# The second node stage of a two-layer graph network on Trainium2: its order of work written out step by step, with rows fetched into six buffers

## The chip, the cores and the metric

The kernel runs on one core of one Trainium2 chip. The metric is device time in microseconds (us). Before the change it is 3491.12 us, the median of three runs from 3474.59 to 3492.3. All times of parts come from one profiled execution of the kernel, whose own time is 3487.8 us and whose span is 3486.0 us.

A core has five engines with a queue of instructions each: PE (matrix multiply, with its weight loads shown as PEld), DVE (vector), ACT (scalar functions), POOL (general purpose, issues the indirect transfers here) and SP (issues transfers).[...]

## The reference, cut to what matters

Two layers of a graph network act on 6250 nodes with 256 features and 100000 edges. The first, `_L0_gnn_ref`, ends with a stage per node, and the second, `_L1_gnn_ref`, begins with one. In the reference, with `t` the mean of the messages at a node and `x` the normalised input:

```python
trans = typed_linear(t, Wa, ba)              # one of 3 matrices, by the node's type
alpha = sigmoid(skip)[node_type][:, None]
out = trans * alpha + x * (1.0 - alpha)
normed = (out - mu) * rsqrt(var + LN_EPS) * ln_g[node_type] + ln_b[node_type]
L0 = where(has_msg, normed, x)
x = x0 + L0                                  # x0: the kernel's input
h = maximum(_layernorm(x), 0.0)              # second layer's input
xw = h @ W                                   # and its two attention sums per head
```

The kernel computes exactly these lines, per block of nodes, in the stage that is changed. After it, the second layer gathers rows of `xw` for every edge.

## The kernel before, in words

**Stages.** A first node stage makes keys, values and queries and writes the table `hq_d`. A first edge stage gathers 832 groups of key and value rows and sums messages into `QA`, an array in SBUF (its first 256 columns are `acc0`). The second node stage, L1342 to L1442, is the one in question. A second edge stage (from L1451) gathers 832 groups of rows of `xw_d`, sums them into `acc1`, and a last stage normalises over all nodes. Each edge stage ends with a part under a run-time condition; at such a condition all engines meet. So the second node stage starts with all engines free, and from there to the end of the second edge stage's fixed part the instructions are one pool that the planner may order.

**The second node stage.** The 6250 nodes are cut into 50 blocks of 127 (`NB`, `BN`). For each block, `block(b)` (L1372) does, in four pieces separated by `yield`:

1. loads rows of `x` into `xbuf` and of `hq_d` into `hbuf` (`load_rows`, L170, two transfers each because 127 rows are cut into 112 and 15); clears and loads a tile with the types of the nodes (`load_types`, L183; POOL memset L187, transfer L188); gathers the three per-type rows (scale, offset, skip) into `norm` (an indirect transfer on POOL, L971, with three buffers); turns the block's message sums with PE (L197) and multiplies them by the mask of each of the three types (`by_type`, L193; DVE, L200, three instructions called `tm`); makes `xh` on ACT (L1384) and adds `x` to it on POOL (L1385).
2. twelve matmul instructions on PE for the six products with `wa_s` (L1390); on DVE the skip term `o` (L1395), `o` plus product (L1396), mean and variance (`norm_stats`, L151: statistics L154 and L156, the square root on ACT L158, the reciprocal on DVE L159), and the two instructions of the normalisation (L1398, L1399).
3. `xn` on DVE (L1402), its statistics, `shift` (L1405), the relu `h2` on ACT (L1407), the sum `r` on POOL (L1409) and its store to `r_d` (SP, L177).
4. two transposes of `h2` (PE, L1414), a copy to SBUF (ACT, L1416), the next layer's rows (PE, four instructions, L1419), three copies (ACT, L1421 to L1424) and the store to `xw_d` (SP).

**What sets the order.** A loop starts one block per round and advances up to three blocks by one piece each, oldest last. This is only the order in which the instructions are handed over. The stage is not under a fixed order: the planner that builds the program orders each engine's instructions by what its own estimate says is ready, and lets later code of the same region move ahead. `xbuf` and `hbuf` have four slots, everything else three (`wk`), and one PSUM pool of eight banks serves all PSUM tiles.

After the loop, DVE turns the attention sums into `es` and `adst` (L1434 to L1442), and the second edge stage begins: `acc1` is cleared on DVE (L1453), and its first gathers (POOL, L971, `rows<-xw_d`) follow.

Of the kernel before, what the change touches and what calls it, by code (L numbers as in the profile page):

```python
# [24 lines left out]
def kernel(  # L25
# [122 lines left out]
    kind_at = pers.tile([P, NB], I32, name="kind_at")  # L148


    def norm_stats(pool, a, tag):  # L151

        st = pool.tile([P, nc.vector.BN_STATS_DIM], F32, name="st_" + tag)
        nc.vector.bn_stats(out=st, in_=a)  # L154
        mv = pool.tile([P, nc.vector.BN_AGGR_DIM], F32, name="mv_" + tag)
        nc.vector.bn_aggr(out=mv, in_=st)  # L156
        rs = pool.tile([P, 1], F32, name="rs_" + tag)
        nc.scalar.activation(rs, mv[:, 1:2], AF.Sqrt, bias=eps_t)  # L158
        nc.vector.reciprocal(rs, rs)  # L159
        return mv[:, 0:1], rs  # L160

    def rows_of(b):
        return LAST if b == NB - 1 else BN

# [5 lines left out]
    def load_rows(t, a, b):  # L170

        for o, e in pieces(rows_of(b)):
            nc.sync.dma_start(t[o + 1 : e + 1], a[b * BN + o : b * BN + e, :])

    def store_rows(a, b, t, eng=None):
        for o, e in pieces(rows_of(b)):
            (eng or nc.sync).dma_start(a[b * BN + o : b * BN + e, :], t[o + 1 : e + 1])  # L177

    def by_block(a, some):

        return a[some, :].rearrange("(b p) d -> p b d", p=BN)

    def load_types(pool, b):  # L183

        t = pool.tile([P, P], I32, name="ntype")
        n = rows_of(b)
        nc.gpsimd.memset(t, -1)  # L187
        nc.sync.dma_start(  # L188
            t[:, 1 : n + 1], bass.AP(tensor=node_type.tensor, offset=node_type.offset + b * BN, ap=[[0, P], [1, n]])
        )  # L190
        return t

    def by_type(pool, psum, a, nt, tag):  # L193

        ps = psum.tile([P, FC, P], F32, name="nps")
        for c in range(FC):
            nc.tensor.transpose(ps[:, c, :], a[:, c * P : (c + 1) * P], ident)  # L197
        m = pool.tile([P, T, FC, P], F32, name=tag)
        for t in range(T):
            nc.vector.scalar_tensor_tensor(  # L200
                m[:, t], nt[:, None, :].to_broadcast([P, FC, P]), float(t), ps, op0=OP.is_equal, op1=OP.mult
            )
        return m

# [765 lines left out]
    def gather(to, table, index):  # L970
        nc.gpsimd.indirect_dma_start(  # L971
            out=to, out_offset=None, in_=table[:, :], in_offset=bass.IndirectOffsetOnAxis(ap=index, axis=0)
        )
# [368 lines left out]
    with ExitStack() as st:  # L1342
        cst = st.enter_context(tc.tile_pool(name="e0c", bufs=1))
        wk = st.enter_context(tc.tile_pool(name="e0w", bufs=3))
        pp = st.enter_context(tc.tile_pool(name="e0p", bufs=8, space=PSUM))
        wa_s = load_w(cst, Wa, "wa_s")


        gw_s = cst.tile([P, FC, D], F32, name="gw_s")
        nc.scalar.dma_start(gw_s, gW.rearrange("(c p) o -> p c o", p=P))  # L1350
        asd = cst.tile([P, 2, D], F32, name="asd")
        nc.scalar.dma_start(asd[:, 0, :], bcast(att_src, D))
        nc.scalar.dma_start(asd[:, 1, :], bcast(att_dst, D))
        gwx = cst.tile([P, FC, H * XW + H], F32, name="gwx")
        by_head = gwx[:, :, : H * XW].rearrange("p c (h e) -> p c h e", h=H)
        for c in range(FC):
            nc.scalar.copy(by_head[:, c, :, :DK], gw_s[:, c, :].rearrange("p (h e) -> p h e", h=H))
            pr = wk.tile([P, 2, H, DK], F32, name="pr")
            nc.vector.tensor_tensor(
                pr.rearrange("p i h e -> p i (h e)"), gw_s[:, c, None, :].to_broadcast([P, 2, D]), asd, op=OP.mult  # L1360
            )
            nc.vector.tensor_reduce(by_head[:, c, :, DK], pr[:, 0], AX.X, OP.add)
            nc.vector.tensor_reduce(gwx[:, c, H * XW :], pr[:, 1], AX.X, OP.add)
        a_sd = cst.tile([P, NB, 2, H], F32, name="a_sd")

        XB = 4
        xbuf = cst.tile([P, XB, D], F32, name="xbuf")
        hbuf = cst.tile([P, XB, D], F32, name="hbuf")
        nc.gpsimd.memset(xbuf, 0.0)
        nc.gpsimd.memset(hbuf, 0.0)  # L1370

        def block(b):  # L1372

            xb = xbuf[:, b % XB, :]
            load_rows(xb, x, b)
            nt = load_types(wk, b)
            hb = hbuf[:, b % XB, :]
            load_rows(hb, hq_d[:, :D], b)
            norm = wk.tile([P, 3, D], F32, name="norm")
            gather(norm.rearrange("p i d -> p (i d)"), norm_d, kind_at[:, b : b + 1])  # L1380
            m = by_type(wk, pp, acc0[:, b, :D], nt, "tm")

            xh = wk.tile([P, D], F32, name="xh")
            nc.scalar.activation(xh, hb, AF.Copy, scale=nhas[:, b : b + 1])  # L1384
            nc.gpsimd.tensor_tensor(xh, xh, xb, op=OP.add)  # L1385
            yield
            tr = pp.tile([P, D], F32, name="nps")
            for t in range(T):
                for c in range(FC):
                    nc.tensor.matmul(  # L1390
                        tr, m[:, t, c, :], wa_s[:, t, c, :],
                        start=(t == 0 and c == 0), stop=(t == T - 1 and c == FC - 1),
                    )
            o = wk.tile([P, D], F32, name="o")
            nc.vector.scalar_tensor_tensor(o, hb, nalpha[:, b : b + 1], norm[:, 2, :], op0=OP.mult, op1=OP.add)  # L1395
            nc.vector.scalar_tensor_tensor(o, tr, share[:, b : b + 1], o, op0=OP.mult, op1=OP.add)  # L1396
            mean, rs = norm_stats(wk, o, "o")
            nc.vector.scalar_tensor_tensor(o, o, mean, norm[:, 0, :], op0=OP.subtract, op1=OP.mult)  # L1398
            nc.vector.scalar_tensor_tensor(o, o, rs, norm[:, 1, :], op0=OP.mult, op1=OP.add)  # L1399
            yield  # L1400
            xn = wk.tile([P, D], F32, name="xn")
            nc.vector.scalar_tensor_tensor(xn, o, has[:, b : b + 1], xh, op0=OP.mult, op1=OP.add)  # L1402
            mean, rs = norm_stats(wk, xn, "x")
            shift = wk.tile([P, 1], F32, name="shift")
            nc.vector.tensor_scalar(shift, mean, rs, -1.0, op0=OP.mult, op1=OP.mult)  # L1405
            h2 = wk.tile([P, D], F32, name="h2")
            nc.scalar.activation(h2, xn, AF.Relu, bias=shift, scale=rs)  # L1407
            r = wk.tile([P, D], F32, name="r")
            nc.gpsimd.tensor_tensor(r, xn, h2, op=OP.add)  # L1409
            store_rows(r_d, b, r)  # L1410
            yield
            hp = pp.tile([P, FC, P], F32, name="nps")
            for c in range(FC):
                nc.tensor.transpose(hp[:, c, :], h2[:, c * P : (c + 1) * P], ident)  # L1414
            hT = wk.tile([P, FC, P], F32, name="hT")
            nc.scalar.copy(hT, hp)  # L1416
            wp = pp.tile([P, H * XW + H], F32, name="nps")
            for c in range(FC):
                nc.tensor.matmul(wp, hT[:, c, :], gwx[:, c, :], start=(c == 0), stop=(c == FC - 1))  # L1419
            xw = wk.tile([P, H, XW], F32, name="xw")  # L1420
            nc.scalar.copy(xw.rearrange("p h e -> p (h e)"), wp[:, : H * XW])  # L1421
            store_rows(xw_d, b, xw.rearrange("p h e -> p (h e)"))
            nc.scalar.copy(a_sd[:, b, 0, :], xw[:, :, DK])
            nc.scalar.copy(a_sd[:, b, 1, :], wp[:, H * XW :])  # L1424

        parts = []
        for b in range(NB + 3):
            if b < NB:
                parts.append(block(b))
            for p in parts[::-1]:  # L1430
                next(p, None)
            parts = parts[-3:]

        es = cst.tile([P, NB, 2 * H], F32, name="es")  # L1434
        nc.vector.tensor_copy(es[:, :, :H], a_sd[:, :, 1, :])
        nc.vector.tensor_add(es[:, :, H:], a_sd[:, :, 0, :], a_sd[:, :, 1, :])
        nc.vector.scalar_tensor_tensor(es[:, :, H:], es[:, :, H:], 0.2, es[:, :, H:], op0=OP.mult, op1=OP.max)
        for i in range(3):
            nc.vector.tensor_copy(adst[:, :, i, :], es)
            if i < 2:  # L1440
                nc.vector.tensor_tensor(es, es, adst[:, :, i, :], op=OP.subtract)
# [463 lines left out]
```

## Time and profile before

The stage lies between 1818 and about 2128 us of the span. For three parts of it (us):

| from : to | PE busy | DVE busy | ACT busy | POOL busy | granted PE clock | DMA share |
|---|---|---|---|---|---|---|
| 1818.0 : 1845.0 | 14.06 | 15.38 | 4.80 | 10.29 | 0.66 | 0.65 |
| 1845.0 : 2100.0 | 201.29 | 209.77 | 111.78 | 121.48 | 0.97 | 0.64 |
| 2100.0 : 2128.7 | 10.03 | 20.83 | 5.61 | 2.27 | 0.60 | 0.08 |

| whole execution | |
|---|---|
| its own time | 3487.8 us |
| span | 3486.0 us |
| median of the runs | 3491.12 us |
| busy in the span | PE 67%, DVE 72%, ACT 54%, POOL 60% |

How to read the lines that follow. A row in order of time gives start, duration, engine, line, operation, `output<-inputs`, shapes, a count, and in brackets how long the engine had been idle and what ended that wait. An engine name with a `q` (SPq, ACTq) is the issuing of a transfer by that engine's queue. Matmuls overlap each other, so a busy PE is not a PE at its peak. Two DVE rows may overlap by about 0.1 us[...].

### The profile page before, as it was taken

The numbers are of one execution on the slowest core, as the hardware profiler recorded it, in microseconds if no ns is written. First come the engines' busy times: TensorE is split into PE (matmuls) and PEld (weight loads), VectorE is DVE, ScalarE is ACT, GpSimd is POOL, SyncE is SP. The second block draws the span as 40 slices with busy tenths as digits, with TensorE's granted clock in tenths as the row PEclk, the third lists the DMA queues.
The fourth block names the chain that finished last, engine by engine and source line by source line (L and its number), as shares of the span: only waits on it lengthen the run. The fifth ranks groups of instructions, "written<-read, shape, count | busy, mean of one in ns | idle before, by whom it ended". The sixth has DMA issues, their size and how long they took to land. (4 is left out here: it accounts for less than half of the span.)

```text
span 3486.0 us, 45931 instructions
## 1 busy us (share of the span) xinstructions
PE 2321.6 (67%) x9879; PEld 1626.8 (47%) x9879; DVE 2501.3 (72%) x5600; ACT 1884.6 (54%) x7331; POOL 2105.7 (60%) x2144
## 2 busy tenths in 40 slices
PE   3888765787777777777767772465555556556680
PEld 2555543555555555555536662344344334434440
DVE  8998705898898988889858884455555555555688
ACT  5665561776677777677764441444444444444511
POOL 4665555676666666666614444777777777777300
PEclk9899887998899999999989995677877877777855
DMA  3555687676666767666626663444444444444224
GB/s 99 232 210 219 205 273 222 202 215 198 196 193 199 210 204 206 193 199 207 197 76 171 178 177 103 127 126 129 126 123 127 125 123 128 125 125 127 56 77 132
DMA packets 263729, 571.80 MB, mean 164 GB/s; under 512 B 66395, under 2 KB 162193, under 8 KB 257194
## 3 DMA queue, kind: packets, MB, share of 16 engines
q0 software_dynamic: 124368, 444.93, 41.9%
q1 hardware_dynamic: 131838, 116.55, 12.3%
q10 hardware_dynamic: 7238, 7.22, 0.8%
q8 instruction: 94, 1.54, 0.2%
q14 instruction: 191, 1.56, 0.1%
HBM read 458.42 MB, written 114.06 MB: 164 GB/s over the span
## 5 line engine op out<-in xcount | busy, mean ns | idle before, releaser
L971 POOL DMA_INDIRECT ring<-kv_d,idx x832 | 820.3, 986 | 438.4 <-ACT wrows L1230 184.7
L971 POOL DMA_INDIRECT rows<-xw_d,idx x832 | 873.2, 1049 | 260.8 <-issue 203.8
L1230 ACT ACTIVATE wrows<-ring,wt 128x64 f32<-128x64 f32 x3328 | 834.2, 335 | 0.1
L1713 PE MATMUL aps<-wrows,ebn 128*128 128x264 f32 x1664 | 605.1, 505 | 301.9 <-DVE ebn L1689 151.4
L1074 PE MATMUL qe<-QA,nbe 128*128 x1664 | 467.6, 415 | 170.7 <-DVE nbe L1059 102.5
L1295 PE MATMUL aps<-wrows,ebn 128*128 128x258 f32 x1664 | 520.4, 422 | 38.9 <-ACT wrows L1230 31.7
L1713 PEld LDWEIGHTS aps<-wrows,ebn 128*128 128x128 f32 x1664 | 350.3, 237 | 383.5 <-ACT wrows L1675 332.9
L1074 PEld LDWEIGHTS qe<-QA,nbe 128*128 128x128 f32 x1664 | 330.5, 207 | 265.4 <-issue 165.6
L1675 ACT ACTIVATE wrows<-rows,ex 128x64 f32<-128x64 f32 x1664 | 434.2, 336 | 0.0
L1295 PEld LDWEIGHTS aps<-wrows,ebn 128*128 128x128 f32 x1664 | 318.2, 206 | 131.3 <-ACT wrows L1230 80.7
L1086 DVE TENSOR_TENSOR pr<-ring,qe 128x512 f32<-128x512 f32 x416 | 277.3, 679 | 133.1 <-PE qe L1074 65.8
L1532 ACT COPY asr<-rows 128x16 f32<-128x16 f32 x208 | 44.8, 216 | 575.1 <-DMA rows<-xw_d,idx 575.1
L1729 DVE TENSOR_TENSOR acc<-acc,aps 128x264 f32 x416 | 176.8, 425 | 192.2 <-PE aps L1713 178.0
L1089 DVE TENSOR_REDUCE att<-pr 128x8 f32<-128x512 f32 x416 | 268.7, 677 | 0.1
L1239 DVE SCALAR_TENSOR_TENSOR QA<-QA,same,aps 128x258 f32 x416 | 194.1, 467 | 43.3 <-PE aps L1295 39.4
L578 ACT COPY QA<-rps 128x768 f32<-128x768 f32 x204 | 163.8, 803 | 88.2 <-PE rps L577 85.2
L1577 DVE TENSOR_TENSOR e<-asr,ad 128x128 f32<-128x128 f32 x26 | 10.1, 388 | 215.1 <-ACT asr L1532 215.1
L1390 PE MATMUL nps<-wa_s,tm 128*128 128x256 f32 x600 | 146.6, 397 | 9.2 <-DMA norm<-norm_d,kind_at 6.4
L447 POOL DMA_INDIRECT kv_d<-QA,to_row x51 | 56.7, 1112 | 148.1 <-ACT QA L578 141.5
L1553 PEld LDWEIGHTS <-near 128*128 128x128 bf16 x832 | 96.8, 118 | 102.1 <-issue 41.9
L1689 DVE TENSOR_TENSOR ebn<-ifree,dl 128x512 f32<-128x512 f32 x208 | 142.7, 686 | 0.0
L1208 DVE TENSOR_TENSOR ebn<-ifree,dl 128x512 f32<-128x512 f32 x208 | 140.7, 676 | 2.8 <-PE aps L1295 2.8
(438 smaller groups left out, 3947.3 us busy)
## 6 DMA issues: line engine op xcount, KB each, us to landing
near<-row_d SPq DMA_DIRECT2D x208, 128.0 KB
near<-row_d SPq DMA_DIRECT2D x52, 512.0 KB
ring<-kv_d,idx POOLq DMA_INDIRECT x832
rows<-xw_d,idx POOLq DMA_INDIRECT x832
keeps<-prev_d SPq DMA_DIRECT2D x416, 16.0 KB
xw_d<-xw SPq DMA_DIRECT2D x49, 113.8 KB
xbuf<-xw_d SPq DMA_DIRECT2D x49, 113.8 KB
xbuf<-in_x_dram SPq DMA_DIRECT2D x49, 112.0 KB
```

The costliest lines, as they stand in the source:

```text
L578: nc.scalar.copy(rel[:, :, i, 2 * c : 2 * c + 2, :].rearrange("p r h e -> p h r e"), ps)
L971: nc.gpsimd.indirect_dma_start(out=to, out_offset=None, in_=table[:, :], in_offset=bass.IndirectOffsetOnAxis(ap=index, axis=0))
L1074: nc.tensor.matmul(qe[:, i, :], oh[j // GT][:, j % GT + i, :], QA[:, 1:, :D][:, bass.ds(bs[j // 2], 1), :].rearrange("p a d -> p (a d)"), ...
L1086: nc.vector.tensor_tensor(pr.rearrange("p t h e -> p t (h e)"), ring[:, lane : lane + 2, slot(t), :], qe, op=OP.mult)
L1089: nc.vector.tensor_reduce(att[:, :, k + j : k + j + 2].rearrange("p h t -> p t h"), pr, AX.X, OP.add)
L1230: nc.scalar.activation(wv[:, j % GT, cols], v[:, cols], AF.Copy, scale=w[:, h, j : j + 1])
L1239: nc.vector.scalar_tensor_tensor(a, a, same[:, t : t + 1], sums.pop(j), op0=OP.mult, op1=OP.add),
L1295: nc.tensor.matmul(sums[j - j % 2], hot[j // GT][:, j % GT, :], wvs[j // GT][:, j % GT, :], start=(j % 2 == 0), stop=(j % 2 == 1),)
L1390: nc.tensor.matmul(tr, m[:, t, c, :], wa_s[:, t, c, :], start=(t == 0 and c == 0), stop=(t == T - 1 and c == FC - 1),)
L1675: nc.scalar.activation(wv[:, part, h, :DK], rows[:, part, h, :DK], AF.Copy, scale=ex[:, 0, h, g * GT + part : g * GT + part + 1],)
L1713: nc.tensor.matmul(sums[t - t % 2], oh[:, t % GT, :], wv[:, t % GT].rearrange("p h e -> p (h e)"), start=(t % 2 == 0), stop=(t % 2 == 1),)
L1729: nc.vector.tensor_tensor(a, a, sums.pop(t).rearrange("p (h e) -> p h e", h=H), op=OP.add)
```

## The change

The stage is put under a fixed order: inside it each engine issues its instructions in the order in which they are written. Where the stage's instructions fall among others of the same engine that are written outside it stays with the planner. The pieces of a block become twelve functions, and a step calls each for another block. Rows, types and per-type rows are fetched three steps ahead into six slots (`tbuf`, `nbuf`, `xbuf`, `hbuf`); the types' slots are cleared once instead of once per block. The PSUM pool has two buffers for each of four tiles instead of eight for all. The reciprocal of each standard deviation moves behind the next DVE instruction(s). The two stores to `xw_d` are issued by ACT instead of SP. The computations themselves, and their shapes, stay.

```diff
-        pp = st.enter_context(tc.tile_pool(name="e0p", bufs=8, space=PSUM))
+        pp = st.enter_context(tc.tile_pool(name="e0p", bufs=2, space=PSUM))
...
-        XB = 4
+        AHEAD = 3
+        XB = AHEAD + 3
...
+        tbuf = cst.tile([P, XB, P], I32, name="tbuf")
+        nbuf = cst.tile([P, XB, 3, D], F32, name="nbuf")
...
+        def fetch_rows(b):
+            i = b % XB
+            n = rows_of(b)
+            nc.sync.dma_start(
+                tbuf[:, i, 1 : n + 1],
+                bass.AP(tensor=node_type.tensor, offset=node_type.offset + b * BN, ap=[[0, P], [1, n]]),
+            )
+            load_rows(hbuf[:, i, :], hq_d[:, :D], b)
+            load_rows(xbuf[:, i, :], x, b)
+            gather(nbuf[:, i].rearrange("p i d -> p (i d)"), norm_d, kind_at[:, b : b + 1])
...
+        def added(b):
+            i = b % XB
+            xh = live["xh", b] = wk.tile([P, D], F32, name="xh")
+            nc.scalar.activation(xh, hbuf[:, i, :], AF.Copy, scale=nhas[:, b : b + 1])
+            nc.gpsimd.tensor_tensor(xh, xh, xbuf[:, i, :], op=OP.add)
...
+        def norm_of(b):
+            i = b % XB
+            o = live["o", b]
+            mean, rs = live.pop(("so", b))
+            nc.vector.scalar_tensor_tensor(o, o, mean, nbuf[:, i, 0, :], op0=OP.subtract, op1=OP.mult)
+            nc.vector.reciprocal(rs, rs)
+            nc.vector.scalar_tensor_tensor(o, o, rs, nbuf[:, i, 1, :], op0=OP.mult, op1=OP.add)
...
+            store_rows(xw_d, b, xw.rearrange("p h e -> p (h e)"), nc.scalar)
...
-        parts = []
-        for b in range(NB + 3):
-            if b < NB:
-                parts.append(block(b))
-            for p in parts[::-1]:
-                next(p, None)
-            parts = parts[-3:]
+        with tc.manual_schedule():
+            for step in range(-AHEAD, NB + 4):
+                for back, part in (
+                    (AHEAD, fetch_rows),
+                    (1, added),
+                    (2, turn_sums),
+                    (1, masks),
+                    (-3, rows_of_next),
+                    (-2, turn_rows),
+                    (1, products),
+                    (1, skips),
+                    (0, sums_in),
+                    (-1, joined),
+                    (0, norm_of),
+                    (-1, rows_out),
+                ):
+                    if 0 <= step + back < NB:
+                        part(step + back)
```

By engine, a step is then: DVE `masks` (three `tm`), `skips`, `sums_in` (the product added to `o`, and its statistics), `joined` (`xn` and its statistics), `norm_of` (two instructions with the reciprocal between), `rows_out` (reciprocal and `shift`). POOL: the gather, the addition of `xh`, the addition of `r`. ACT: `xh`, the copy `xw` with its two stores, two small copies, the copy `hT`, two square roots, the relu. PE: `turn_sums`, `rows_of_next`, `turn_rows`, `products`. SP: five loads and the two stores to `r_d`.

More of the change, by code (lines that the diff above doesn't have):

```diff
@@ L148 @@
     kind_at = pers.tile([P, NB], I32, name="kind_at")
[L151 to L160, printed above, removed]
     def rows_of(b):
@@ L181, in by_block @@
         return a[some, :].rearrange("(b p) d -> p b d", p=BN)
[L183 to L203, printed above, removed]
     qapool = tc.tile_pool(name="qapool", bufs=1)
@@ L1364, with turn_sums, masks, products @@
         a_sd = cst.tile([P, NB, 2, H], F32, name="a_sd")
-        XB = 4
+        AHEAD = 3
+        XB = AHEAD + 3
         xbuf = cst.tile([P, XB, D], F32, name="xbuf")
         hbuf = cst.tile([P, XB, D], F32, name="hbuf")
+        tbuf = cst.tile([P, XB, P], I32, name="tbuf")
+        nbuf = cst.tile([P, XB, 3, D], F32, name="nbuf")
         nc.gpsimd.memset(xbuf, 0.0)
         nc.gpsimd.memset(hbuf, 0.0)
[L1372 to L1387, printed above, removed]
+        nc.gpsimd.memset(tbuf, -1)
+        live = {}
+        def fetch_rows(b):
[8 more added lines that the diff above has]
+            gather(nbuf[:, i].rearrange("p i d -> p (i d)"), norm_d, kind_at[:, b : b + 1])
+        def turn_sums(b):
+            ps = live["sums", b] = pp.tile([P, FC, P], F32, name="sums_ps")
+            for c in range(FC):
+                nc.tensor.transpose(ps[:, c, :], acc0[:, b, c * P : (c + 1) * P], ident)
+        def masks(b):
+            ps = live.pop(("sums", b))
+            m = live["tm", b] = wk.tile([P, T, FC, P], F32, name="tm")
+            nt = tbuf[:, b % XB, :]
+            for t in range(T):
+                nc.vector.scalar_tensor_tensor(
+                    m[:, t], nt[:, None, :].to_broadcast([P, FC, P]), float(t), ps, op0=OP.is_equal, op1=OP.mult
+                )
+        def products(b):
+            m = live.pop(("tm", b))
+            tr = live["tr", b] = pp.tile([P, D], F32, name="tr_ps")
             for t in range(T):
@@ L1393, in block @@
                     )
[L1394 to L1403, printed above, removed]
+        def skips(b):
+            i = b % XB
+            o = live["o", b] = wk.tile([P, D], F32, name="o")
+            nc.vector.scalar_tensor_tensor(
+                o, hbuf[:, i, :], nalpha[:, b : b + 1], nbuf[:, i, 2, :], op0=OP.mult, op1=OP.add
+            )
+        def added(b):
[3 more added lines that the diff above has]
+            nc.gpsimd.tensor_tensor(xh, xh, xbuf[:, i, :], op=OP.add)
@@ new lines, in spread, with sums_in @@
+        def spread(a, tag):
+            st_ = wk.tile([P, nc.vector.BN_STATS_DIM], F32, name="st_" + tag)
+            nc.vector.bn_stats(out=st_, in_=a)
+            mv = wk.tile([P, nc.vector.BN_AGGR_DIM], F32, name="mv_" + tag)
+            nc.vector.bn_aggr(out=mv, in_=st_)
+            rs = wk.tile([P, 1], F32, name="rs_" + tag)
+            nc.scalar.activation(rs, mv[:, 1:2], AF.Sqrt, bias=eps_t)
+            return mv[:, 0:1], rs
+        def sums_in(b):
+            o = live["o", b]
+            nc.vector.scalar_tensor_tensor(
+                o, live.pop(("tr", b)), share[:, b : b + 1], o, op0=OP.mult, op1=OP.add
+            )
+            live["so", b] = spread(o, "o")
@@ new lines, in norm_of, with joined @@
+        def norm_of(b):
+            i = b % XB
+            o = live["o", b]
+            mean, rs = live.pop(("so", b))
+            nc.vector.scalar_tensor_tensor(o, o, mean, nbuf[:, i, 0, :], op0=OP.subtract, op1=OP.mult)
+            nc.vector.reciprocal(rs, rs)
+            nc.vector.scalar_tensor_tensor(o, o, rs, nbuf[:, i, 1, :], op0=OP.mult, op1=OP.add)
+        def joined(b):
+            xn = live["xn", b] = wk.tile([P, D], F32, name="xn")
+            nc.vector.scalar_tensor_tensor(
+                xn, live.pop(("o", b)), has[:, b : b + 1], live.pop(("xh", b)), op0=OP.mult, op1=OP.add
+            )
+            live["sx", b] = spread(xn, "x")
@@ L1404, in block, with rows_out @@
+        def rows_out(b):
+            xn = live.pop(("xn", b))
+            mean, rs = live.pop(("sx", b))
+            nc.vector.reciprocal(rs, rs)
             shift = wk.tile([P, 1], F32, name="shift")
             nc.vector.tensor_scalar(shift, mean, rs, -1.0, op0=OP.mult, op1=OP.mult)
-            h2 = wk.tile([P, D], F32, name="h2")
+            h2 = live["h2", b] = wk.tile([P, D], F32, name="h2")
             nc.scalar.activation(h2, xn, AF.Relu, bias=shift, scale=rs)
@@ L1410, in block, with turn_rows, rows_of_next @@
             store_rows(r_d, b, r)
-            yield
-            hp = pp.tile([P, FC, P], F32, name="nps")
+        def turn_rows(b):
+            h2 = live.pop(("h2", b))
+            ps = pp.tile([P, FC, P], F32, name="rows_ps")
             for c in range(FC):
[L1414 to L1417, printed above, removed]
+                nc.tensor.transpose(ps[:, c, :], h2[:, c * P : (c + 1) * P], ident)
+            hT = live["hT", b] = wk.tile([P, FC, P], F32, name="hT")
+            nc.scalar.copy(hT, ps)
+        def rows_of_next(b):
+            hT = live.pop(("hT", b))
+            wp = pp.tile([P, H * XW + H], F32, name="next_ps")
             for c in range(FC):
@@ L1421, in block @@
             nc.scalar.copy(xw.rearrange("p h e -> p (h e)"), wp[:, : H * XW])
-            store_rows(xw_d, b, xw.rearrange("p h e -> p (h e)"))
+            store_rows(xw_d, b, xw.rearrange("p h e -> p (h e)"), nc.scalar)
             nc.scalar.copy(a_sd[:, b, 0, :], xw[:, :, DK])
             nc.scalar.copy(a_sd[:, b, 1, :], wp[:, H * XW :])
-        parts = []
-        for b in range(NB + 3):
-            if b < NB:
-                parts.append(block(b))
-            for p in parts[::-1]:
-                next(p, None)
-            parts = parts[-3:]
+        with tc.manual_schedule():
[16 more added lines that the diff above has]
+                        part(step + back)
         es = cst.tile([P, NB, 2 * H], F32, name="es")
```

## The prediction

> **What bounds it now.** I read the stage table first, then the waits, then one step in order of time. For 1868.54 to 2097.39 us of the stage the profile says:
>
> ```profile
> 1868.54:2097.39 228.85, 179.22 (x843) 145.76 (x841) 190.23 (x631) 100.48 (x336) 109.78 (x166) 0.99 0.65 177
> ```
>
> The columns are length, then busy us of PE, PE load, DVE, ACT and POOL, granted clock, DMA share, GB/s. `xn` (L1402) starts at 1868.54 and, 42 blocks on, at 2097.39: 5.45 us per block, DVE busy 190.23/42 = 4.53 of it. So no engine is full. The waits from 1850 to 2080 name a ring:
>
> ```profile
> DVE o L1395 <- DMA norm<-norm_d,kind_at: 36.7, 41, 2.3
> POOL norm L971 <- DVE o L1399: 31.6, 31, 1.6
> ```
>
> In order of time (start, duration, engine):
>
> ```profile
> 1948.43 0.21 DVE L1405 TENSOR_SCALAR shift<-mv_x,rs_x 128x1 f32<-128x1 f32 x1
> ...
> 1949.41 0.72 POOL L1409 TENSOR_TENSOR r<-xn,h 128x256 f32<-128x256 f32 x1 [1.14 <-ACT h L1407]
> ...
> 1949.72 0.70 DVE L1395 SCALAR_TENSOR_TENSOR o<-hbuf,nalpha,norm 128x256 f32<-128x256 f32 x1 [0.61 <-DMA norm<-norm_d,kind_at]
> 1950.34 0.47 DVE L1399 SCALAR_TENSOR_TENSOR o<-o,rs_o,norm 128x256 f32<-128x256 f32 x1
> ...
> 1950.74 1.07 DVE L200 SCALAR_TENSOR_TENSOR tm<-ntype,nps 128x256 f32<-128x256 int32 x3
> 1951.08 0.96 POOL L971 DMA_INDIRECT norm<-norm_d,kind_at  x1 [0.95 <-DVE o L1399]
> ```
>
> The three `norm` buffers close a ring: L1399 frees one (1950.81), the gather starts 0.27 later, runs 0.96, its rows are there about 3 us on, L1395 waits for them at the head of DVE's queue, and L1399 stands behind it. That gives the 5.27 between most steps, and more when the rows are late.
>
> **What is removed.** Six row buffers filled three steps ahead take the gather off the ring: a row is asked for two steps (over 9 us) before its first use, against about 4 us from gather to use. The stall on `norm`, 36.7 us in 230, goes. The memset of the types (0.22 of POOL per block) goes too. The clearing of the larger buffers costs POOL some 1.5 us once.
>
> **What DVE then needs.** I lay one step out in the new order. Start-to-start times are from the trace: 0.99 for three `tm`, 0.40 behind an independent scalar-tensor-tensor, 0.51 and 0.47 where the next reads the result:
>
> ```profile
> 1857.60 0.48 DVE L1402 SCALAR_TENSOR_TENSOR xn<-o,has,xh 128x256 f32<-128x256 f32 x1
> 1858.11 0.43 DVE L154 BATCH_NORM_STATS2 st_x<-xn 128x6 f32<-128x256 f32 x1
> 1858.58 0.18 DVE L156 BATCH_NORM_AGGREGATE mv_x<-st_x 128x2 f32<-128x6 f32 x1
> ```
>
> masks 0.99, skips 0.40, sums_in 0.51 + 0.46 + 0.11, joined 0.51 + 0.46 + 0.12, norm_of 0.39 + 0.20 + 0.39, rows_out 0.20 + 0.13: **4.87 us**. (The old order slips another block's instruction between dependent ones: 4.40 without its stall. The new one pays 0.47 for dependent neighbours.)
>
> A rule to weigh here is the Trainium skill's "VectorE: DVE Perf Modes", section "The DRAIN you can't avoid": an op starts only when the pipe of the one before is empty. Taken so, both orders cost the sum of durations, for the new one about 5.4. The rows show independent neighbours 0.08 to 0.09 early (1949.72 + 0.70 ends after 1950.34), so I use the starts.
>
> **What speaks against it: POOL's two additions.** L1385 and L1409, 0.72 each, read two SBUF inputs. So do four DVE ops of a step: skips, joined and the two of norm_of. L1395 above took 0.70 instead of its undisturbed 0.48: the addition ended at 1950.13, L1395 0.29 later. Every overlap in this stage fits "end of the addition + 0.28". The other way:
>
> ```profile
> 1955.59 0.48 DVE L1399 SCALAR_TENSOR_TENSOR o<-o,rs_o,norm 128x256 f32<-128x256 f32 x1
> 1955.60 1.06 POOL L1409 TENSOR_TENSOR r<-xn,h 128x256 f32<-128x256 f32 x1 [2.05 <-ACT h L1407]
> ```
>
> DVE was 0.01 earlier and POOL ended 0.59 after it. L1396 and `tm`, which read PSUM, and the statistics are not lengthened by an addition. The skill has this as a rule against such a packing ("SBUF — State Buffer", section "SBUF: two separate sides"): a DVE op with two SBUF inputs and a GpSimd op that reads SBUF share an exclusive lock; who starts first keeps it for the whole instruction. The rows agree on who waits, but a held op ends 0.28 after the addition, not a whole 0.48: with the rule's wording each collision would cost 0.20 more. I use the rows.
>
> In the old order the additions fell mostly beside statistics or into the stall. The new order has no stall for them to fall into, so where they fall decides:
>
> - *r of the block before.* With `tm` at 0, shift ends at 0.08, the relu (0.60, starting 0.04 on) at 0.72, and the addition (0.08 on) runs 0.80 to 1.53. Skips starts at 0.99, is held and ends at 1.53 + 0.28 = 1.81 in place of 1.47: **+0.34**. The margin is 0.19, so I take this as certain.
> - *xh.* Behind that addition in POOL's order stands the gather: 0.15 to start, 0.96, to 2.64. The addition of xh runs 2.65 to 3.37. The delayed DVE has sums_in at 1.73, its statistics at 2.24 and 2.71, and joined at 2.82: held to 3.65 in place of 3.30, **+0.35**. The margin is only 0.17: a gather slower by that lets joined go first, and this part costs nothing.
> - norm_of then starts at 4.26, clear of both.
>
> So a step is 4.87 + 0.34 + 0.35 = **5.56 us**, against 5.45 now.
>
> **The other queues.** PE: 2.46 for twelve loads of products, 0.36 + 0.36 for the transposes, 0.74 for the next layer's rows, 3.95 per step at full clock, in any order. It waits for the h2 of the step before at about 0.8, and products end near 3.7, 3 us before sums_in of the next step wants them: hidden. If the clock fell to 0.70, PE would be level with DVE. ACT: 2.8 of its own plus two DMA issues moved to it from SP. ACT's own issues in this stage's start are 0.35 to 0.48, so 0.8: about 3.9 with its waits, under 5.56. Queued behind them are hT and both square roots, which DVE waits for. They have some 1.6 to spare, so an issue would have to cost 1.2. SP: seven issues of about 0.42, 2.9. It waits at r's store until 1.6 of the next step, with the fetch for three blocks on queued behind; that fetch lands 7 to 8 us later, needed at 11. Transfers take 0.65 x 5.45 = 3.5 us of the DMA engines per block. All hidden.
>
> **Start and end.** The start stays bound by the same 1.3 MB of weights and the same preparation on DVE up to 1835.5. From there: masks and skips of the second block 1.4, the first one's sums_in and statistics to 1838.4, ACT's table load and root (1.28 + 0.29, as now) and norm_of to 1840.6, masks, skips and sums_in of the next step 2.5: the first `xn` at 1843.1 (1842.09 now, then slow steps up to 1868.54 for the sixth). The sixth of the new order falls at 1843.1 + 5 x 5.56 = 1870.9, +2.4. At the end:
>
> ```profile
> 2100.57 11.06 DVE L1453 MEMSET acc<- 128x13200 f32 x1 [2.70 <-issue]
> 2111.55 0.36 DVE L1396 SCALAR_TENSOR_TENSOR o<-nps,share,o 128x256 f32<-128x256 f32 x1
> ...
> 2128.67 0.99 POOL L971 DMA_INDIRECT rows<-xw_d,idx  x1 [7.60 <-DVE es L1441]
> ```
>
> The next layer's memset sits inside this stage, 11 us before the last blocks; the next stage's gathers start behind `es`, 31.3 after the 48th `xn`, and pace what follows. In the new order the rest after the 48th `xn` is 2.7 + 3.5 for two emptying steps, 10.3 for the last block's chain through ACT, PE (at half clock there, as now) and es: 16.5. The memset is not part of the fixed order, so it can still fall in between (+11.06 = 27.6) or behind the last block's DVE work (22.4). Gain 3.7 to 8.9; I take 3.7.
>
> Sum: +2.4 at the start, 42 x 0.11 = +4.6, -3.7 at the end: **+3.3 us** on the profiled execution's 3487.8, so 3491.1. That execution is 3.3 below the median of the runs shown, so 3494 in their terms with the memset inside, 3489 behind; I say **3491**. Half a per cent, about what a measurement of this kernel can tell from no change, is 17 us.
>
> **Rivals.**
> - *One collision only (20%).* If joined starts before xh's addition, a step is 5.21: 42 x -0.24 = -10, about +1 at the start, -4 at the end: 3475. For it: the thin margin, and gathers of 1.1 to 1.4 elsewhere in the trace. Against: in this stage they hold 0.96.
> - *No collision (20%).* The additions fall beside statistics and masks: 4.87, 42 x -0.58 = -24, -1 and -4: 3458 to 3462. This is the change doing all that taking the ring away can do. For it: 0.19 of margin is small. Against: the relu starts the addition at a fixed distance from `tm`.
> - *ACT's queue becomes the bound (12%).* An issue that is held on ACT blocks the roots behind it. With DMA busy, SP's issues for `xbuf` took 3.08 and 3.14 for two at 1823 and 1829. At 1.54 each, ACT needs 3.1 + 3.1 = 6.2 per step: 42 x 0.75 = +31, 3520. It decides from 1.2 per issue. Against: in the steady part SP's are 0.31 to 0.45 at the same DMA share.
> - *The likeliest (48%)*, both collisions: 3485 to 3500.
>
> Chances: faster by over 0.5% 0.24 (no collision, and the faster edge of one), within 0.5% 0.63, slower 0.13. The range, 3458 to 3502, leaves out the slower rival and a little of the fastest.
>
> **What would show it.** In the profile after: no DVE wait on `norm`; `xn` every 5.5 us; skips and joined at about 0.8 in place of 0.48, each ending 0.28 after an addition on POOL; DVE busier (over 5 us per step); ACT's issues near 0.4. A step of 4.9 with both at 0.48 would refute the collisions, 5.2 the second. Steps over 5.8 with DVE waiting for ACT's roots would mean the ACT queue. A memset outside the stage would move the end by 5 to 11 us alone.

## The result and the profile after

The changed kernel takes 3500.58 us (median of 20 runs, 3486.96 to 3511.56), the kernel before 3490.59 in the same comparison (20 runs): a ratio of **1.004, 95% interval 1.0028 to 1.0052** (the quotient of the two medians alone is 1.0029, inside that interval). The forecast was 3491, no change; the kernel is slower by 0.3 to 0.5%. The profiled execution after spans 3495.8 us, against 3486.0 before.

The stage from 1850 to 2080 us in the profile after, by windows (length, then busy us of PE, PE load, DVE, ACT, POOL, then granted clock, DMA share, GB/s):

```profile
1850.00:2080.00 230.00, 170.01 (x822) 135.64 (x821) 221.22 (x616) 97.02 (x329) 99.86 (x124) 1.00 0.69 176
```

DVE, 83% busy before, is now 96% busy, and the kernel is not faster: the time has moved from waiting into "busy". The waits of that stretch, longest first:

```profile
PEld rows_ps L1443 <- ACT h L1434: 77.0, 41, 2.2
POOL r L1436 <- ACT h L1434: 62.5, 21, 3.0
POOL r L1436 <- DMA hbuf<-hq_d: 48.5, 16, 3.0
```

No row says that DVE waits for `nbuf`. The ring is gone: 36.7 us of it. PE and POOL wait for work, which costs nothing while DVE is 96% busy. (POOL's wait ahead of `r` is for the relu, also where a row names a transfer of `hbuf`: in the step below the relu ends at 1953.86 and the addition starts at 1953.93.) Where DVE's busy time grew is in the groups of the same stretch, one per line, operation and shape (busy us, mean ns of one, then idle us ahead of them). First `skips` and `joined` in the kernel before, then the groups after:

```profile
L1395 DVE SCALAR_TENSOR_TENSOR o<-hbuf,nalpha,norm 128x256 f32<-128x256 f32 x42 | 24.6, 586 | 36.7 <-DMA norm<-norm_d,kind_at 36.7
...
L1402 DVE SCALAR_TENSOR_TENSOR xn<-o,has,xh 128x256 f32<-128x256 f32 x41 | 19.4, 474 | 0.0
```

```profile
L1422 DVE SCALAR_TENSOR_TENSOR xn<-o,has,xh 128x256 f32<-128x256 f32 x42 | 36.9, 878 | 0.0
L1385 DVE SCALAR_TENSOR_TENSOR o<-hbuf,nalpha,nbuf 128x256 f32<-128x256 f32 x41 | 35.1, 857 | 0.0
...
L1418 DVE SCALAR_TENSOR_TENSOR o<-o,rs_o,nbuf 128x256 f32<-128x256 f32 x41 | 19.9, 485 | 1.5
...
L1416 DVE SCALAR_TENSOR_TENSOR o<-o,mv_o,nbuf 128x256 f32<-128x256 f32 x41 | 18.8, 459 | 0.0
```

Four operations of one kind and size: after the change two take 0.46 to 0.49 us, `skips` (L1385) and `joined` (L1422) nearly twice that. One step in order of time says why (start, duration, engine):

```profile
1952.95 0.21 DVE L1432 TENSOR_SCALAR shift<-mv_x,rs_x 128x1 f32<-128x1 f32 x1
1953.08 1.07 DVE L1368 SCALAR_TENSOR_TENSOR tm<-tbuf,sums_ps 128x256 f32<-128x256 int32 x3
1953.26 0.60 ACT L1434 ACTIVATE h<-xn,shift,rs_x 128x256 f32<-128x256 f32 x1 [1.05 <-DVE shift L1432]
1953.93 0.73 POOL L1436 TENSOR_TENSOR r<-xn,h 128x256 f32<-128x256 f32 x1 [3.03 <-DMA hbuf<-hq_d]
1954.07 0.87 DVE L1385 SCALAR_TENSOR_TENSOR o<-hbuf,nalpha,nbuf 128x256 f32<-128x256 f32 x1
1954.81 0.97 POOL L938 DMA_INDIRECT nbuf<-norm_d,kind_at  x1
...
1955.79 0.74 POOL L1394 TENSOR_TENSOR xh<-xh,xbuf 128x256 f32<-128x256 f32 x1
...
1955.93 0.89 DVE L1422 SCALAR_TENSOR_TENSOR xn<-o,has,xh 128x256 f32<-128x256 f32 x1
```

POOL's addition of `r` ends at 1954.66, L1385 0.28 later. POOL's addition of `xh` ends at 1956.53, L1422 0.29 later. Both collisions are there in nearly every step.

The stage cut at three points, from POOL's first memset of `xbuf` to the first gather of the second edge stage, in the two profiled executions:

| stretch | before | after | difference | forecast |
|---|---|---|---|---|
| start to the 6th `xn` | 50.3 | 49.5 | -0.8 | +2.4 |
| a step, 6th to 46th `xn` | 5.458 | 5.611 | +0.15 (40 steps: +6.1) | +0.11 |
| 46th `xn` to the gather | 41.8 | 45.0 | +3.2 | about -3 |
| the stage | 310.5 | 319.0 | +8.5 | +3.3 |

So the stage carries 8.5 of the 9.8 us by which the spans differ. The steady step went as forecast, a little more so; the end did not.

```profile
2095.68 11.06 DVE L1496 MEMSET acc<- 128x13200 f32 x1 [2.70 <-issue]
2106.65 0.36 DVE L1418 SCALAR_TENSOR_TENSOR o<-o,rs_o,nbuf 128x256 f32<-128x256 f32 x1
...
2135.98 0.96 POOL L938 DMA_INDIRECT rows<-xw_d,idx  x1 [9.79 <-DVE firsts L1519]
```

The memset stands inside the fixed order, between two instructions of one block's `norm_of`, again with 2.70 us of idle ahead of it.

### The profile page after: what moved, and what is told of

Same layout as the page of the kernel before. It is cut to its first block, busy times and chain, and to the rows that moved or that the text cites. A ratio compares the mean times of both kernels' runs of the same rounds, so it can differ in the third digit from the quotient of the medians.

```text
span 3495.8 us, 45769 instructions
## 1 busy us (share of the span) xinstructions
PE 2309.7 (66%) x9879; PEld 1612.2 (46%) x9879; DVE 2545.1 (73%) x5600; ACT 1883.3 (54%) x7331; POOL 2099.0 (60%) x2095
## 3 DMA queue, kind: packets, MB, share of 16 engines
q8 instruction: 94, 1.54, 0.2%
## 5 line engine op out<-in xcount | busy, mean ns | idle before, releaser
L1377 PE MATMUL tr_ps<-wa_s,tm 128*128 128x256 f32 x600 | 143.4, 390 | 9.0 <-DMA xbuf<-in_x_dram 8.2
L1725 DVE TENSOR_TENSOR wrows<-rows,ex 128x512 f32<-128x512 f32 x208 | 142.0, 683 | 0.4
```

The source lines that it names most:

```text
L1377: nc.tensor.matmul(tr, m[:, t, c, :], wa_s[:, t, c, :], start=(t == 0 and c == 0), stop=(t == T - 1 and c == FC - 1),)
```

## The experiments

The theory: the two collisions make the step, and the end is lengthened by the memset with its idle time and by ACT's stores. Rivals: the fixed order itself (dependent neighbours on DVE) costs what the ring did; ACT's queue is the bound; the transfers are. Each ratio is to the kernel before in the same comparison: 3496.13 us for e1 to e4, 4001.03 for e5 to e8, 3491.25 for e9 and e10. e5 to e8 were on another chip, on which the edge stages take longer (the stage begins at 2172 in e5, at 1817 in after); the stage's DVE durations are the same on both. So times are compared by their ratios, and sizes inside the stage by the profiles. Step, end (46th `xn` to the gather) and stage are from the profiles, in us:

| kernel | step | end | stage | time | ratio to before, 95% |
|---|---|---|---|---|---|
| before | 5.46 | 41.8 | 310.5 | 3490.59 | 1 |
| after | 5.61 | 45.0 | 319.0 | 3500.58 | 1.0040 (1.0028 to 1.0052) |
| e1 additions only write | 4.81 | 44.5 | 282.4 | 3455.6 (one run) | - |
| e2 skips ahead of masks | 5.00 | 44.6 | 293.3 | 3471.13 | 0.9931 (0.9907 to 0.9955) |
| e3 old order, six `norm` buffers | 4.84 | 40.6 | 280.7 | 3466.46 | 0.9921 (0.9896 to 0.9946) |
| e4 stores on SP | 5.63 | 42.7 | 316.9 | 3500.62 | 1.0014 (1.0002 to 1.0025) |
| e5 memset last | 5.62 | 31.5 | 306.2 | 3999.15 | 0.9994 (0.9972 to 1.0015) |
| e6 e3 with memset last | 4.90 | 27.2 | 270.4 | 3967.97 | 0.9911 (0.9876 to 0.9946) |
| e8 e2 with `xh` ahead of the gather | 4.95 | 43.8 | 288.5 | 3979.38 | 0.9943 (0.9922 to 0.9963) |
| e7 interleaved order | 4.95 | 26.1 | 269.5 | 3956.83 | 0.9892 (0.9848 to 0.9935) |
| e9 e7 with stores on ACT | 4.90 | 30.6 | 274.8 | 3452.04 | 0.9886 (0.9865 to 0.9906) |
| e10 e7, six gathers only | 4.40 | 26.8 | 245.8 | 3430.6 (one run) | - |

**e1, the additions replaced by memsets.** POOL writes as long as it added, and reads nothing:

```
-            nc.gpsimd.tensor_tensor(xh, xh, xbuf[:, i, :], op=OP.add)
+            nc.gpsimd.memset(xh3, 0.5)
...
-            nc.gpsimd.tensor_tensor(r, xn, h2, op=OP.add)
+            nc.scalar.copy(r3[:, 0, :1], h2[:, :1])
+            nc.gpsimd.memset(r3, 0.5)
```

> The changed kernel with both POOL additions replaced by clearing a tile three times as wide (about 0.75 us, writes only, reads no SBUF; a one-column copy on ACT keeps r's clear behind the relu). Left out: the sums xh + x and xn + h2, so the second layer and the output get constants there. Theory (an addition on POOL and a DVE op with two SBUF inputs shut each other out): skips falls from 0.88 to 0.48 and joined from 0.89 to 0.45, a step from 5.63 to about 4.8, although POOL is as busy. Rival 1 (the fixed order itself, with its dependent neighbours on DVE, is what costs): the step stays at 5.6. Rival 2 (a busy POOL slows DVE whatever it does): the step stays above 5.4.

One step of it in order of time:

```profile
1954.33 0.48 DVE L1385 SCALAR_TENSOR_TENSOR o<-hbuf,nalpha,nbuf 128x256 f32<-128x256 f32 x1
1954.39 0.74 POOL L1438 MEMSET r<- 128x768 f32 x1 [2.20 <-ACT r L1437]
...
1955.80 0.45 DVE L1423 SCALAR_TENSOR_TENSOR xn<-o,has,xh 128x256 f32<-128x256 f32 x1
...
1956.23 0.75 POOL L1395 MEMSET xh<- 128x768 f32 x1
```

The step is 4.81: the fixed order without the collisions, dependent neighbours and all, costs 0.65 less than the old order with its ring. The rival "the order itself" falls for the step. Both DVE operations are back at their undisturbed 0.48 and 0.45, and the memset of `r`, which starts 0.06 behind `skips`, keeps its 0.74 (an addition that starts so close behind such an operation takes 1.0, see e3). The small copy on ACT put POOL's work some 0.2 us later, so e1 alone does not show that it is the reading, and not the place, that collides. e2 moves the place.

**e2, skips ahead of the masks.** Everything else stays:

```
                     (2, turn_sums),
+                    (1, skips),
                     (1, masks),
...
-                    (1, skips),
```

> The changed kernel with one line moved: skips stands ahead of masks in a step. Theory: skips runs 0 to 0.48, before r's addition begins (0.85 after the step's start); that addition then lies beside the three tm, which read PSUM; joined starts at 2.47 and is now ahead of xh's addition (2.7), which waits for it. Both collisions go: a step of 4.8 to 4.9, 45 x 0.75 = 34 us less than the changed kernel, about 3465 or 0.993 of the kernel before. Rival (the collisions only move, to norm_of or the reciprocals): step 5.2 to 5.6, 3482 to 3500.

The step is 5.00, between the expected 4.8 to 4.9 and the rival's 5.2; the stage is 25.7 us shorter than after's. `skips` takes 0.48, and the addition of `r` now runs beside `tm` and `sums_in`, which read PSUM and are not lengthened (0.41 and 0.48). `joined` takes 0.64, not 0.45, though it starts first:

```profile
1965.01 0.96 POOL L938 DMA_INDIRECT nbuf<-norm_d,kind_at  x1
...
1965.74 0.64 DVE L1422 SCALAR_TENSOR_TENSOR xn<-o,has,xh 128x256 f32<-128x256 f32 x1
1965.99 0.97 POOL L1394 TENSOR_TENSOR xh<-xh,xbuf 128x256 f32<-128x256 f32 x1
```

POOL's addition waits and ends 0.58 after DVE's, as in the case of before in which DVE was first. What the 0.19 of DVE itself is, this run left open; e8 is made for it.

**e3, only the buffers, in the old order.**

```
-            norm = wk.tile([P, 3, D], F32, name="norm")
+            norm = wk.tile([P, 3, D], F32, name="norm", bufs=6)
```

> The kernel before with six norm buffers in place of three, the planner's order otherwise. Theory: the ring of gather, L1395, L1399 opens and DVE's wait on norm (36.7 us in 230) goes; what is left is 4.4 per step plus what the additions on POOL then hit, 4.4 to 5.2, so 10 to 45 us less than before (0.987 to 0.997). Rival (the next wait lies close behind, rows of hbuf and xbuf or ACT's xh): the step stays within 0.1 of 5.45 and the time within 0.2%.

One number in one line gives 0.9921. In the first 24 of the 40 steps the length alternates between 4.34 and 4.95, 4.65 in the mean; in every second one the addition of `r` falls on L1399, which then takes 0.77 to 0.82 instead of 0.48. In the last 16 steps, with waits for `hbuf`, the mean is 5.14. Windows of the two parts:

```profile
1871.36:1982.83 111.47, 100.41 (x481) 81.93 (x480) 108.31 (x361) 59.88 (x192) 69.25 (x96) 1.00 0.77 207
1982.83:2065.08 82.25, 67.16 (x323) 54.81 (x322) 74.58 (x241) 38.30 (x128) 44.76 (x64) 1.00 0.70 189
```

Over all 40 steps the ring was worth 0.61 a step, and the change gave all of it back. The undisturbed steps, 4.34 here and 4.80 in e1, also give the price of dependent neighbours in the new order: 0.46. And this run has the overlap in which DVE is first:

```profile
1905.02 0.47 DVE L1395 SCALAR_TENSOR_TENSOR o<-hbuf,nalpha,norm 128x256 f32<-128x256 f32 x1
1905.26 0.81 POOL L1385 TENSOR_TENSOR xh<-xh,xbuf 128x256 f32<-128x256 f32 x1 [0.23 <-DMA hbuf<-hq_d]
```

In all 46 such cases of this profile, 0.05 to 0.46 ahead, the DVE operation keeps its 0.47 to 0.48, and the addition waits (0.81 here, 1.00 where DVE is 0.06 ahead).

**e4, the stores to `xw_d` on SP again.** `nc.scalar` is taken out of that one call.

> The changed kernel with the stores to xw_d issued by SP again. Theory: in the steady part ACT has time to spare, the step stays 5.63; at the end, where the last block's chain runs alone, ACT's roots and copies no longer stand behind two issues of 0.4: the distance from the last xn to the first gather of rows falls from 14.4 to about 11.5, the time by 3 us (0.999 of the changed kernel, 1.003 of the one before). Rival (ACT's issues gate the step): the step falls below 5.4.

The step does not change (5.63), so ACT's queue is no bound of the steady part. The end is 2.3 us shorter in the profile, the stage 2.1. The ratio falls from 1.0040 to 1.0014, by more than 2.1 us would make it (0.06%); the stage does not show where the rest is. In after's last blocks nothing covers ACT:

```profile
2126.17 0.38 ACT L1453 COPY xw<-next_ps 128x260 f32<-128x260 f32 x1 [0.79 <-PE next_ps L1451]
2126.58 0.86 ACTq L166 DMA_DIRECT2D xw_d<-xw  x2
...
2127.64 0.38 ACT L1445 COPY hT<-rows_ps 128x256 f32<-128x256 f32 x1
2128.06 2.13 PE L1451 MATMUL next_ps<-gwx,hT 128*128 128x264 f32 x4 [1.50 <-ACT hT L1445]
```

The copy `hT`, which the last block's matmuls wait for, stands behind 0.86 us of ACT's own queue (the ACTq row; 0.82 of it are the two issues themselves).

**e5, the memset behind `es`.** DVE's order is fixed from the first `es` operation to the memset of `acc1`:

```
+        at_end = tc.manual_schedule(engines={mybir.EngineType.DVE})
+        at_end.__enter__()
         es = cst.tile([P, NB, 2 * H], F32, name="es")
...
     nc.vector.memset(acc1, 0.0)
+    at_end.__exit__(None, None, None)
```

> The changed kernel, with VectorE's large memset (11.06 us, and 2.70 us idle in front of it) put behind the es and adst operations in VectorE's order; the six-step order is untouched. Theory: the end after the 46th xn is bare, so the whole 13.8 us comes out of it; next stage VectorE idles 24 us before its first scores, which covers the memset. End 45.0 -> 31.2 us, step unchanged at 5.6, time about 3487, that is 0.999 of the kernel before. Rival: the next stage waits for the near comparison behind the memset, or the gather waits for it, and the time stays at 3500, 1.003 to 1.005.

```profile
2478.53 0.96 POOL L938 DMA_INDIRECT rows<-xw_d,idx  x1 [9.85 <-DVE adst L1484]
...
2480.30 11.06 DVE L1498 MEMSET acc<- 128x13200 f32 x1 [2.70 <-DMA keeps<-prev_d]
```

The end is 31.5, 13.5 less than after's 45.0: 11.06 and the 2.70 of idle both, since the idle time goes where the memset goes. The step is after's. The ratio is 0.9994; after itself was not run on this chip, so the size rests on the profiles. This run also corrects a reading: after's row names `firsts` (L1519) as what the gather waited for. Here `firsts` comes behind the memset, 12 us later, and the gather starts at the same 4.28 us behind the start of `es` as in after (3.2 to 3.3 in the old order). It was not `firsts`. The row above names the last copy into `adst` instead, and the traces agree: in all nine profiles of the fixed order the gather starts 0.92 to 0.93 after that copy has ended, in the three of the old order (before, e3, e6) 0.05 to 0.17 before its end. So the extra 1.0 us is a wait for that copy; why the planner's program has it in one order and not in the other is not shown.

**e6, e3 with the same memset edit.**

> The kernel before with six norm buffers and the same memset put behind es and adst. Theory: both gains add, since one is in the step and one in the end: step 4.84, end 40.6 - 13.8 = 27, stage 267 us, time about 3466 - 14 = 3452, 0.988 of the kernel before. Rival: the planned order had the memset beside waits already, and the gain is a few us only (3460, 0.991).

End 27.2, stage 270.4: the end fell as e5's did, by 13.4. The step was 4.90 instead of 4.84, which takes back 2.4. The ratio is the rival's, 0.9911, only a little better than e3's and with overlapping intervals: what the stage gained is not seen in the whole time, and this run does not say why.

**e8, `xh` ahead of the gather, on top of e2.** `added` is handed over before `fetch_rows`, so POOL adds before it gathers.

> The changed kernel with skips ahead of the masks and the xh addition ahead of the fetches (so ahead of GpSimd's gather). Theory: xh is added some 1.1 us earlier, while VectorE is at the PSUM operations and at the statistics; joined falls from 0.64 to 0.45-0.48 and the step from 5.00 to 4.80; time about 3463, 0.992. Rival: the remaining 0.19 us of joined is not from the addition beside it; the step stays at 5.0 and the time at 3471.

```profile
2303.01 0.73 POOL L1394 TENSOR_TENSOR xh<-xh,xbuf 128x256 f32<-128x256 f32 x1
...
2303.89 0.96 POOL L938 DMA_INDIRECT nbuf<-norm_d,kind_at  x1
2303.93 0.46 DVE L1422 SCALAR_TENSOR_TENSOR xn<-o,has,xh 128x256 f32<-128x256 f32 x1
```

`joined` is 0.45, with the gather running beside it: the 0.19 in e2 is not the price of a gather alone. The expected step of 4.80 is there, in 25 of the 40 steps between the 6th and the 46th `xn`; the others go up to 5.88, and the mean is 4.95, so the ratio is no better than e2's. Something else had come up. A slow step in order of time, with the transfer that matters in it:

```profile
2299.50 0.35 SPq L1349 DMA_DIRECT2D tbuf<-in_node_type_dram  x1
...
2302.93 2.69 ACTq L166 DMA_DIRECT2D xw_d<-xw  x2
2305.30 0.33 ACTq L166 DMA_DIRECT2D xw_d<-xw  x1
2305.66 0.20 ACT L1455 COPY a_sd<-xw 128x4 f32<-128x4 f32 x1 [2.76 <-DMA tbuf<-in_node_type_dram]
...
2306.42 0.16 DVE L1417 RECIPROCAL rs_o<-rs_o 128x1 f32<-128x1 f32 x1 [0.99 <-ACT rs_o L1402]
```

The second ACTq row is the second of the two stores by itself. It takes 0.33, and the first 0.31: the 2.69 us are not issuing, there are 2.05 us of waiting between the two. The trace has what was waited for. The nine transfers that SP and ACT issue per step signal their landing through eight semaphores, taken in turn, and an issue waits until the earlier transfer on its semaphore has landed. The second store shares one with the load of `tbuf` issued at 2299.50, which landed at 2305.28. Behind the store stood the square root that DVE waits for. In the waits from 2250 to 2380 this is ACT's longest:

```profile
ACT a_sd L1455 <- DMA tbuf<-in_node_type_dram: 39.5, 25, 2.8
```

This is the third rival of the prediction, at a faster step, but not by the price of an issue: the two issues of a pair take 0.64 together in the median, with 0.70 between them; in after it was 0.76 with 0.04.

**e7, two blocks' dependent operations in turn.** The fixed order is kept; `sums_in`, `joined`, `norm_of` and `rows_out` are cut into their operations and taken in the order below. Stores on SP, memset last:

```
                    (1, added),
                    (AHEAD, fetch_rows),
                    (1, skips),
...
                    (0, sums_in),
                    (0, stats_o),
                    (-1, joined),
                    (0, moments_o),
                    (-1, stats_x),
                    (0, norm_a),
                    (0, root_o),
                    (-1, moments_x),
                    (0, norm_b),
                    (-1, root_x),
                    (-1, rows_out),
```

> Fixed order as in the changed kernel, but VectorE's dependent operations of two blocks taken in turn (sums, statistics of o, joined, moments of o, statistics of xn, first norm operation, root, moments of xn, second norm operation, root, shift), skips ahead of the masks, the xh addition ahead of the gather, the xw stores on SyncE, the memset last. Theory: no collision and few dependent neighbours, so the step comes near the 4.40 us that the planned order's VectorE work took without its stall: 4.4 to 4.6, end about 31, stage about 258, time about 3440, 0.985. Rival: TensorE (4.15 us busy a step) or ScalarE's chain of roots becomes the bound, or an addition collides again: step 4.8 or more, time 3455 or more, 0.990.

Ratio 0.9892. An undisturbed step is the expected 4.40, and no operation of the kind of `skips` is lengthened in the median; but the mean is 4.95, the rival's number, though not for a cause that the rival names. Its windows and its DVE waits from 2250 to 2380:

```profile
2250.00:2380.00 130.00, 112.94 (x520) 88.50 (x519) 115.25 (x390) 62.96 (x208) 63.90 (x78) 0.97 0.80 197
```

```profile
DVE o L1385 <- DMA hbuf<-hq_d: 12.8, 15, 2.3
```

DVE waits for rows whose fetch is written three steps ahead. SP comes to it late: in the trace it issues the loads of `hbuf` 4.3 us before `skips` starts (median; 9.3 in after), and they land 3.8 us later, up to 5.7. Either SP, with nine issues a step, asks too late, or the rows take too long.

**e9 and e10 tell these two apart.** e9 is e7 with the two stores on ACT (SP issues seven). e10 is e7 with

```
+            if b < XB:
                 gather(nbuf[:, i].rearrange("p i d -> p (i d)"), norm_d, kind_at[:, b : b + 1])
```

> The interleaved order with the stores to xw_d on ScalarE's queue, as in the changed kernel: SyncE issues seven DMAs a step instead of nine. If SyncE's issuing is what made the interleaved order's step 4.95 us where its VectorE work takes 4.40, the step falls to 4.4-4.6 and the time to 0.985 of the kernel before. Rival: the transfers themselves (about 1.0 MB a step, 198 GB/s in every kernel whose step is below 5 us) are the bound; then the step stays at 4.9 to 5.0 and only the place of the waits changes, with ScalarE's issues stretched and ScalarE's own work behind them.

> The interleaved order with the norm rows gathered for the first six blocks only; later blocks use the rows that are in the buffers, so the values are not the reference's. SyncE issues what it issued; some 0.39 MB a step are not moved. If the transfers are the bound, the rows land in time again and nearly all steps are 4.40 us. Rival: SyncE's nine issues a step are the bound; the step stays above 4.8, with VectorE waiting for hbuf as often as before.

e9's step is 4.90, as its rival says. SP now asks for `hbuf` 5.8 us ahead, and DVE no longer waits for it but for roots behind ACT's second store, which waits for a landing as in e8 (0.63 us between the two in the median, up to 2.60). In its windows, 1900 to 2030, the traffic is 199 GB/s (197 in e7's):

```profile
1900.00:2030.00 130.00, 111.55 (x529) 87.58 (x529) 116.78 (x398) 60.51 (x211) 67.20 (x80) 1.00 0.76 199
```

```profile
DVE rs_o L1439 <- ACT rs_o L1405: 11.1, 12, 2.0
```

e10's step is 4.40 in all 40 steps (4.40 or 4.41), with SP issuing as many DMAs as in e7; the loads of `hbuf` land after 3.3 us, 3.8 at most:

```profile
1900.00:2030.00 130.00, 122.34 (x592) 97.39 (x590) 127.96 (x445) 70.20 (x236) 41.04 (x58) 1.00 0.58 133
```

So the number of SP's issues alone is not it. With the gathered rows gone (and POOL's 0.96 us a step of issuing them, but POOL had about half of its time free) the other transfers land sooner, and the waits for them vanish. The next limit of this stage is thus how soon its transfers land: the waits between issues and DVE's waits for rows keep e7 and e9 at 4.95 and 4.90 where their DVE needs 4.40. Two things remain open. Whether the amount of data, the gathers' many rows or the eight semaphores in turn is what counts, no run separates. And a fixed limit of 4.8 to 4.9 us or of some 200 GB/s is not shown: e1 moved 205 GB/s at a step that its DVE alone makes 4.80, and e3's first 24 steps took 4.65 at 207.

## Why the prediction was right and where it failed

- *The ring goes:* right. No DVE wait for `nbuf`.
- *DVE's step without collisions, 4.87:* 4.81 in e1, 4.80 in most steps of e8. The starts were the right measure. Taken by the Trainium skill's "VectorE: DVE Perf Modes", section "The DRAIN you can't avoid", as the prediction weighed it, the durations add up to 5.4, against 4.80 measured. The same section adds that a next operation which is not held starts earlier; the independent neighbours here do, by 0.08 to 0.09.
- *Two collisions, +0.34 and +0.35:* both there, each ending 0.28 to 0.29 after the addition, but +0.39 and +0.44 (0.87 and 0.89 against e1's 0.48 and 0.45). The relu starts 0.10 after `shift` ends, not 0.04, and POOL's chain is later by that; a held operation ends where POOL says, so each 0.05 on POOL is 0.05 on DVE. The Trainium skill's "SBUF — State Buffer", section "SBUF: two separate sides", has who waits; a whole operation behind each addition would, as an estimate from the prediction's sum, have made the step 5.56 + 0.40 = 5.96, against 5.63 measured, so the rows were the better size. The sum: 4.80 + 0.83 = 5.63; measured 5.63 in a regular step, 5.61 in the mean; forecast 5.56. In 40 steps that is 2 us. The step came this close because the undisturbed part was 0.07 too high and the collisions 0.14 too low, which is partly luck.
- *The rivals' prices* held as well (3475 and 3520 are counted from the profiled 3487.8, not from the median). "No collision", 4.87 and 3458 to 3462: e1, 4.81 and 3455.6. "One collision", 5.21 and 3475: e2, 5.00 and 3471, with a collision of half the size. ACT's queue: not in the changed kernel (e4), but it came up in e8 and e9, when the step was short enough. Its unit was misread: the 3.08 us at 1823 are not two issues of 1.54 but 0.90 and 0.33 with 1.84 between them, in which the second waited for a load of `wa_s` to land.
- *Transfers hidden:* right at 5.6 us a step, at a DMA share of 0.69. At DVE's 4.40 they were not hidden: e7 and e9 stayed at 4.95 and 4.90, and e10 without the gathered rows took 4.40.
- *The start, +2.4:* measured -0.8. The first `xn` came 22.0 after the stage's start, against 23.9 before; the forecast had it later than before. The miss is in the first `xn`, forecast at 24.9; the five steps behind it went as forecast (27.5 against 27.8). Its cause is open, and it hid 3.2 us of the miss at the end.
- **The end, -3.7, is the step that failed: its sum was too small.** From the 48th `xn` I had 16.5 for the chain and 11.06 for the memset, after two steps of 5.56: 38.7 from the 46th `xn`, about 3 less than before. Measured were 45.0, 3.2 more than before. Three terms were left out. The 2.70 us of idle ahead of the memset stood in the line that the prediction itself quotes, and goes with it (e5: 13.5, not 11). ACT's two stores are hidden in a step but bare in the emptying chain: 2.3 (e4). And the gather starts 4.3 after the start of `es`, not 3.2, because it now waits for the last copy into `adst`: 1.0 (e5). With about 0.9 more in the chain, not explained, and 0.5 less in the two steps ahead of it, that is the 6.3.

With the end's +6.3, the start's -3.2 and the step's +2 the sum for the stage would have been about +8.4, where 8.5 was measured and +3.3 forecast: slower, by less than half a per cent. The memset did fall inside the stage, for which the prediction's own sum said 3494; the 3491 lay between that and the other case. And twenty runs of each kernel told a change of 0.4% from none, finer than the half per cent that the prediction counted on. The answer to "why no gain from removing a 36.7 us stall" is shown from two sides: e2 and e8 move the additions and get the gain back; e3 takes the ring away in the old order and gets it at once. That the two collisions cost just about what the ring had cost is a coincidence of this order.

## What to carry to other kernels

When a stall is removed from a tight order, look at what fell into the stall: here POOL's two-input additions, which then held VectorE for about as long as the wait had been. Place such additions beside operations that read PSUM or beside statistics, and order the rest of that engine's queue for it. In a chain that empties at a stage's end nothing hides an issue, a memset or its idle time: sum that part instruction by instruction, with the idle that the row shows. And before a long row of a queue is read as the price of issuing, look at its issues one by one: the time can be a wait between them.

## Hardware behaviour that was not expected

- The memset of 128 x 13200 has 2.69 to 2.81 us of DVE idle ahead of it in all twelve profiles, wherever it stands and whatever is named as the releaser. The cause is not shown. Where nothing covers it, its price was 13.5 and 13.4 us (e5, e6), not 11.06.
- In e2 the DVE operation that started 0.25 ahead of POOL's addition still took 0.64 instead of 0.45, and the addition 0.97 instead of 0.73; so in all 44 such cases there. In e3 a DVE operation that was first kept its 0.47 to 0.48 in all 46 cases, in e6 in 43 of 44 (the other was ahead by only 0.04 and was held). What is different in e2 is that the addition starts 0.02 behind the end of a gather. A gather's end alone lengthened nothing (41 `xn` of the kernel before, 0.47 to 0.48). Why the two together do is open.
- An issue can wait for a transfer that its data has nothing to do with: the program gives the nine transfers of a step eight landing semaphores in turn. The two issues of a pair of stores on ACT did not stretch with traffic (0.76 together at 176 GB/s in after, 0.64 at 199 in e8 and e9); the wait between them grew, from 0.04 in the median to 0.70 and 0.63, with single ones over 2. Whatever stands behind them on that engine waits as well.
